# A two-layer graph network on one Trainium2 core: moving the low halves of two split operands ahead, and giving half of the last tile's evictions to ScalarE

## The chip, the cores and the metric

The kernel runs on one core of one Trainium2 chip. The engines that matter here are TensorE (PE in the profile, with its weight loads as PEld), VectorE (DVE), ScalarE (ACT) and GpSimd (POOL); SyncE (SP) issues most of the transfers. Each engine has its own queue of instructions, in the order in which the program emits them; an instruction may have to wait for the results of others, and those behind it on its engine wait with it. The metric is the time of one execution on the device in microseconds (us). The kernel before takes 777.34 us as the median of three runs.

## What is computed

Two graph layers over 2048 nodes, 8 batches and 64 channels, each followed by a residual and a layer norm. `A` is a sparse, row-normalised adjacency matrix.

```python
# layer 0: Chebyshev terms x, Ax, 2A(Ax) - x, mixed by weights that differ from node to node
w   = einsum('nd,dkio->nkio', embedding, weight)      # d = 16, k = 3
x_g = einsum('knm,bmc->bnkc', [I, A, 2AA - I], x)
x   = layernorm(x + einsum('bnki,nkio->bno', x_g, w) + embedding @ bias)
# layer 1: x, Ax, 2A(Ax) - x (twice, with the same A) through one shared weight
x   = layernorm(x + concat([x, Ax, 2AAx - x, Ax, 2AAx - x]) @ W + b)
```

The node-dependent weight is never formed. The kernel multiplies the three terms of a tile of 128 nodes by all 16 weight matrices at once, and then adds the 16 products, each scaled with the node's own embedding value.

## The kernel before

**The stages.** The two hops of layer 0 come first (226 us), then the mixing stage (316 us), which is what the change is about, and last the two hops of layer 1 (234 us). The first product of the first hop of layer 1 follows directly on the last tile of the mixing stage.

**The mixing stage** runs over 16 tiles of 128 nodes, `t` = 0 to 15 (the loop at line 819). A tile has two groups `g` of batches and four groups `dg` of weight matrices: eight pieces, called (0,0) to (1,3) here. For each piece `mix0` (line 393) emits 36 matmuls (line 415) into one buffer `pm` of the accumulator memory, and four scaled evictions that empty that buffer: pieces (0,0) and (1,0) by ScalarE into a buffer `aside` (line 425), whose four parts GpSimd then adds up (line 430), and the six other pieces by VectorE straight into the tile's sum `acc` (line 427). At (1,2) and at the end of the tile GpSimd adds the asides to `acc` (line 399). The tile's layer norm follows: VectorE takes the sum over channels (line 361), GpSimd subtracts the mean (364), ScalarE squares (352), VectorE sums the squares and refines a reciprocal root (369, 333 to 344), GpSimd multiplies (373).

**The accumulator memory** is four buffers (`bank`, line 84) that serve in turn for the eight pieces and for the transposes and projections between them. A piece can start only when the buffer it is given has been emptied. In the program as built, piece (0,0) of a tile gets the buffer of piece (1,2) of the tile before, and piece (0,1) that of (1,3); both are emptied by VectorE.

**The operands of a piece.** An fp32 factor is split into a high half (rounded by ScalarE, line 312), a low half (VectorE: source minus high half, line 314) and a mixed term (ScalarE scales, line 318, and GpSimd adds, line 319). `parts` (line 309) is a generator that does this in two steps: high half; then low half and mixed term. `operands(t)` (line 693) sets it up for the three factors of tile `t`: `of_x` from a transfer `xt` (line 696), `of_hop` from a transpose of `z[1][t]` on TensorE (line 710), `of_second` from `z[2][t]` (line 713), which `times_r` on GpSimd must have scaled before (line 683).

**The order around a tile** is written out by hand: the list `at[g, dg]` holds what is emitted just ahead of a piece's matmuls, and so ahead of its evictions. In tile `t` the factors of tile `t + 1` are prepared: hop at (0,2), x at (0,3) and (1,0), second at (1,1) and (1,2). The layer norm of tile `t - 1` is worked off at (0,2) and (0,3); its result is transposed at (1,3) and projected after the last piece (`project`, line 434: 16 matmuls at line 442, six copies by ScalarE at line 451). Only then does the next tile's first VectorE work come, the sum over channels.

**The last tile** (t = 15) has no next factors. In their place `early` (line 810) prepares steps 0 to 4 of the first product of the next stage: a high half (ScalarE, line 234), a low half (VectorE, line 238), a load of a matrix block (lines 607 to 613, by the helper at 123) and, for steps 0 and 1, its conversion by ScalarE (line 620). The projection of tile 14 comes between pieces (1,2) and (1,3).

**The pools.** The asides, the third factor's parts and the loaded blocks share five buffers ("raw"); the first two factors' parts share four ("s") with the converted blocks; the high halves have eight ("hl"), the transfers `xt` two.

## Time and profile before

| what | us |
|---|---|
| median of three runs (lowest, highest) | 777.34 (777.04, 777.93) |
| the profiled execution, its own time | 777.52 |
| its span, from the first to the last instruction | 775.6 |
| of it the stage 226.2 to 541.9 (mixing) | 315.7 |
| in that stage: PE / PEld / DVE / ACT / POOL busy | 309.8 / 305.3 / 271.2 / 153.1 / 218.3 |
| mean granted TensorE clock, share of full speed | 0.998 |

Spans and instruction times below are those of the profiled execution, which took 0.18 us more than the median. In a list of instructions the columns are start, duration, engine, line, operation, output and inputs, and, in brackets, the idle time of the engine ahead of it and who ended it. The ends of matmuls are modelled, so their starts say more than their durations.

### The profile page before, as it was taken

The page shows a single profiled execution, that of the slowest core. Times are in us where ns is not written, and L with a number is a line of the kernel's source. Part 1 is how long each engine was busy: PE and PEld are TensorE (multiplying, and loading weights), DVE is VectorE, ACT ScalarE, POOL GpSimd, SP SyncE. Part 2 cuts the span into 40 slices and gives each one's busy share as a digit, 9 for nine tenths or more (in the row PEclk, how much of TensorE's full clock was granted, in tenths as well). Part 3 has the DMA queues.
Part 4 walks back from the last instruction along what each step waited for, and adds up shares of the span by engine and source line. Part 5 has one row for each costly group of instructions (what it writes and reads, how often), then busy time and mean ns, then how long its engine had stood idle before and what let it go on. Part 6 is the DMA issues. An engine that isn't in the chain of part 4 may idle for free.

```text
span 775.6 us, 17992 instructions
## 1 busy us (share of the span) xinstructions
PE 761.5 (98%) x7246; PEld 675.2 (87%) x7246; DVE 590.7 (76%) x1230; ACT 386.5 (50%) x752; POOL 251.1 (32%) x245
## 2 busy tenths in 40 slices
PE   9999999999999999999999999999999999999996
PEld 6888888888889999999999999999888888888885
DVE  6778766677748888888888888888678747768663
ACT  4446443877753555544445444445787664112111
POOL 0000000000036777777777777763100000012341
PEclk9999999999999999999999999999999999999999
DMA  9998995655510000000000000011454444565731
GB/s 315 379 399 284 333 315 182 183 156 169 167 42 16 17 15 16 15 16 15 17 16 16 16 16 15 2 30 42 143 163 143 136 150 143 170 190 158 216 129 45
DMA packets 73546, 96.77 MB, mean 125 GB/s; under 512 B 4848, under 2 KB 48368, under 8 KB 73328
## 3 DMA queue, kind: packets, MB, share of 16 engines
q1 hardware_dynamic: 62048, 76.66, 31.5%
q10 hardware_dynamic: 11408, 18.89, 6.5%
q8 instruction: 59, 0.97, 0.5%
q14 instruction: 31, 0.25, 0.1%
HBM read 76.65 MB, written 18.87 MB: 123 GB/s over the span
## 4 chain that ended last, share of the span: by engine, by line
PE 69%; DVE 26%; issue 4%; POOL 0%; ACT 0%; DVEq 0%; POOLq 0%
PE accT L632 26%; DVE acc L427 18%; PE acc L254 15%; PE pm L415 10%; PE a L254 9%; PE accT L254 6%; DVE parts L314 3%; DVE ln_v L333 2%; DVE ss L369 1%; PE accT L782 1%; PE first L143 1%; DVE ln_q L341 0%; DVE ln_q L342 0%; DVE ln_r L344 0%; DVE ln_r L338 0%
## 5 line engine op out<-in xcount | busy, mean ns | idle before, releaser
L415 PE MATMUL pm<-wh,hl 64*128 64x256 f32 x1536 | 240.9, 286 | 5.9 <-DVE acc L427 5.9
L415 PE MATMUL pm<-wm,parts 64*128 64x256 f32 x1536 | 235.9, 280 | 0.0
L415 PE MATMUL pm<-wl,parts 64*128 64x256 f32 x1536 | 235.9, 280 | 0.0
L632 PE MATMUL accT<-s,hl 128*128 128x512 f32 x896 | 205.7, 390 | 0.0
L427 DVE SCALAR_TENSOR_TENSOR acc<-pm,pack_sb,acc 128x256 f32<-128x256 f32 x384 | 185.1, 482 | 26.3 <-PE pm L415 14.2
L632 PEld LDWEIGHTS accT<-s,hl 128*128 128x128 f32 x896 | 167.5, 188 | 35.4 <-issue 0.2
L415 PEld LDWEIGHTS pm<-wh,hl 64*128 64x128 f32 x1536 | 165.2, 188 | 10.6 <-DVE acc L427 8.8
L415 PEld LDWEIGHTS pm<-wl,parts 64*128 64x128 f32 x1536 | 165.2, 187 | 0.0
L415 PEld LDWEIGHTS pm<-wm,parts 64*128 64x128 f32 x1536 | 165.0, 187 | 0.0
L620 ACT CAST s<-raw 128x1024 fp32r<-128x1024 bf16 x104 | 109.7, 1055 | 38.2 <-ACT hl L234 23.5
L254 PE MATMUL acc<-hl,s 128*128 128x512 f32 x512 | 117.1, 390 | 0.0
L254 PEld LDWEIGHTS acc<-hl,s 128*128 128x128 f32 x512 | 95.7, 188 | 21.4 <-DVE hl L238 0.7
L683 POOL TENSOR_TENSOR z<-z,rrow 128x512 f32<-128x512 f32 x16 | 21.0, 1318 | 212.4 <-DVE z L656 212.4
L425 ACT ACTIVATE aside<-pm,pack_sb 128x256 f32<-128x256 f32 x128 | 50.3, 476 | 67.7 <-PE pm L415 67.7
L234 ACT CAST hl<-z 128x256 fp32r<-128x256 f32 (+1 forms) x96 | 47.5, 511 | 64.0 <-PE acc L254 23.4
L430 POOL TENSOR_TENSOR aside<-aside 128x512 f32<-128x512 f32 x64 | 69.8, 1090 | 16.2 <-ACT aside L425 13.7
L254 PE MATMUL a<-hl,s 128*128 128x512 f32 (+1 forms) x352 | 73.4, 370 | 0.0
L254 PEld LDWEIGHTS a<-hl,s 128*128 128x128 f32 x352 | 61.9, 188 | 11.3
L319 POOL TENSOR_TENSOR parts<-parts 128x512 fp32r<-128x512 f32 x45 | 58.0, 1289 | 16.6 <-DVE parts L314 16.0
L238 DVE TENSOR_TENSOR hl<-z,hl 128x512 fp32r<-128x512 f32 (+1 forms) x96 | 53.0, 559 | 10.6 <-ACT hl L234 8.0
L287 POOL TENSOR_TENSOR z<-z,got 128x512 f32<-128x512 f32 x3 | 4.8, 1622 | 143.8 <-ACT got L286 143.8
L254 PE MATMUL accT<-hl,s 128*128 128x512 f32 x192 | 44.3, 390 | 0.0
(129 smaller groups left out, 829.6 us busy)
## 6 DMA issues: line engine op xcount, KB each, us to landing
raw<-in_adj SPq DMA_DIRECT2D x59, 512.0 KB, 5.7
raw<-sums_of SPq DMA_DIRECT2D x64, 256.0 KB, 2.9
sums_of<-z ACTq DMA_DIRECT2D x16, 512.0 KB, 6.2
raw<-quarters SPq DMA_DIRECT2D x32, 256.0 KB, 2.8
raw<-in_adj SPq DMA_DIRECT2D x16, 384.0 KB, 3.4
quarters<-seen ACTq DMA_DIRECT2D x16, 256.0 KB, 5.6
xt<-in_xT SPq DMA_DIRECT2D x16, 256.0 KB, 2.8
z<-in_x SPq DMA_DIRECT2D x15, 256.0 KB, 6.9
```

The costliest lines, as they stand in the source:

```text
L234: ordered(nc.scalar.copy(to[0], src))
L238: ordered(nc.vector.tensor_tensor(to[1], src, to[0], ALU.subtract))
L254: nc.tensor.matmul(accs[i], lhsT=s[:, i * P : (i + 1) * P], rhs=hl[h], start=(first and h == 0), stop=(last and h == 1),)
L314: ordered(nc.vector.tensor_tensor(view(low), src, view(high), ALU.subtract))
L319: ordered(nc.gpsimd.tensor_tensor(mixed, mixed, low, ALU.add))
L415: nc.tensor.matmul(pm[:, j, i], lhsT=tt[k][n][q, 2 * g + i, :], rhs=w_parts[n][k][q, ds, :], start=(k == 0 and n == 0), stop=(k == 2 and n ...
L425: ordered(nc.scalar.activation(aside[g][:, d], got, AF.Copy, scale=e))
L427: ordered(nc.vector.scalar_tensor_tensor(part, got, e, part, ALU.mult, ALU.add))
L430: ordered(nc.gpsimd.tensor_tensor(aside[g][:, :n], aside[g][:, :n], aside[g][:, n : 2 * n], ALU.add))
L620: ordered(nc.scalar.copy(s, got["raw"]))
L632: nc.tensor.matmul(acc[i][:, c], lhsT=hl[h][:, i * P : (i + 1) * P], rhs=S[:, c * 512 : (c + 1) * 512], start=(kk == 0 and h == 0), stop=( ...
L683: ordered(nc.gpsimd.tensor_tensor(to, to, r, ALU.mult))
```

## The change

Three things are changed, all in the mixing stage.

1. `parts` yields once more, between the low half and the mixed term. The transfer `xt` of tile `t + 2` is issued at (1,0) of tile `t`; its high half (ScalarE) and low half (VectorE) are emitted after the projection at the end of tile `t`, ahead of that tile's sum over channels; its mixed term follows at (0,1) of tile `t + 1`. Tile 0 does all three steps for tile 1 at its piece (0,1).
2. The high half of the second factor is emitted at (0,3) instead of (1,1), its low half and mixed term at (1,0) instead of (1,2). The hop factor stays at (0,2).
3. In the last tile pieces (0,1) and (1,1) are evicted by ScalarE too (`on_act=2`): into a second aside, which GpSimd adds to the first. The first aside is added to `acc` ahead of (1,0). The second and third step of tile 14's norm come one piece later, the high and low halves of steps 0 to 4 are emitted at (0,1), (0,2), (0,3), (1,0) and (1,1), the loads of steps 2 to 4 are left to the next stage's own schedule, and the result of tile 14 is transposed at (1,2) instead of (1,3).

```diff
--- before.py
+++ after.py
@@ -312,6 +312,7 @@
         ordered(nc.scalar.copy(view(high), src))
         yield
         ordered(nc.vector.tensor_tensor(view(low), src, view(high), ALU.subtract))
+        yield
         if quick:
             ordered(nc.vector.scalar_tensor_tensor(mixed, high, 1.0 / SPLIT, low, ALU.mult, ALU.add))
         else:
@@ -390,7 +391,7 @@
             ))
         return acc
 
-    def mix0(t, tt, acc, at):
+    def mix0(t, tt, acc, at, on_act=1):
 
         aside = [None, None]
 
@@ -398,10 +399,13 @@
             part = acc[:, 4 * g : 4 * g + 4, :]
             ordered(nc.gpsimd.tensor_tensor(part, part, aside[g][:, 0], ALU.add))
 
+        def summed(one, other, n):
+            ordered(nc.gpsimd.tensor_tensor(one[:, :n], one[:, :n], other, ALU.add))
+
         for g in range(2):
             part = acc[:, 4 * g : 4 * g + 4, :]
             for dg in range(D // DG):
-                if (g, dg) == (1, 2):
+                if (g, dg) == (1, 2 if on_act == 1 else 0):
                     add_aside(0)
                 for work_here in at.get((g, dg), ()):
                     work_here()
@@ -416,18 +420,23 @@
                                     pm[:, j, i], lhsT=tt[k][n][q, 2 * g + i, :], rhs=w_parts[n][k][q, ds, :],
                                     start=(k == 0 and n == 0), stop=(k == 2 and n == 2),
                                 )
-                if dg == 0:
-                    aside[g] = rawp.tile([P, DG, B // 2, C], F32, tag="raw", name="aside")
+                if dg < on_act:
+                    to = rawp.tile([P, DG, B // 2, C], F32, tag="raw", name="aside")
                 for d in range(DG):
                     dd = dg * DG + d
                     got, e = pm[:, :, :, d, :].rearrange("p j i c -> p (j i) c"), emb_sb[:, t, dd : dd + 1]
-                    if dg == 0:
-                        ordered(nc.scalar.activation(aside[g][:, d], got, AF.Copy, scale=e))
+                    if dg < on_act:
+                        ordered(nc.scalar.activation(to[:, d], got, AF.Copy, scale=e))
                     else:
                         ordered(nc.vector.scalar_tensor_tensor(part, got, e, part, ALU.mult, ALU.add))
-                if dg == 0:
-                    for n in (2, 1):
-                        ordered(nc.gpsimd.tensor_tensor(aside[g][:, :n], aside[g][:, :n], aside[g][:, n : 2 * n], ALU.add))
+                if dg < on_act:
+                    if dg == 0:
+                        aside[g] = to
+                    else:
+                        summed(aside[g], to, DG)
+                    if dg == on_act - 1:
+                        for n in (2, 1):
+                            summed(aside[g], aside[g][:, n : 2 * n], n)
         add_aside(1)
         return layernorm(acc)
 
@@ -807,48 +816,56 @@
 
     third_got = {}
 
-    def early(i, least=0):
+    def early(i, *kinds):
 
         got = third_got.setdefault(i, {})
         for lead, part in sorted(third[i], key=lambda part: -part[0]):
-            if lead > least:
+            if part.__name__ in kinds:
                 part(got)
-        third[i] = [part for part in third[i] if part[0] <= least]
-
-    tt, acc, h, norm = first_tile[0], first_tile[5], None, None
+        third[i] = [part for part in third[i] if part[1].__name__ not in kinds]
+
+    def go(it):
+        return lambda: next(it)
+
+    y, s = ("y_high", "y_low"), ("load_sum", "operands")
+    acc, h, norm = first_tile[5], None, None
+    tt = first_tile[0]
+    coming = operands(1)
     for t in range(NT):
         got, last = {}, t == NT - 1
         at = {(g, dg): [] for g in range(2) for dg in range(D // DG)}
+        n1, n2, n3 = [lambda: next(norm)] * 3 if t else [nothing] * 3
 
         if not last:
-            got["tt"], of_x, of_hop, of_second = operands(t + 1)
+            following, of_x, of_hop, of_second = coming
             of_hop = of_hop()
-            at[0, 2] += [lambda it=of_hop: next(it), lambda: next(norm) if t else None, lambda it=of_hop: next(it)]
+            at[0, 1] += [go(of_x)] * (1 if t else 3)
+            at[0, 2] += [go(of_hop), n1, go(of_hop), go(of_hop), n2]
             if t + 2 < NT:
                 at[0, 2] += [lambda: times_r(t + 2)]
-            at[0, 3] += [lambda it=of_x: next(it), lambda: got.update(acc=begin_sum(t + 1))]
-            at[1, 0] += [lambda it=of_x: next(it)]
-            at[1, 1] += [lambda it=of_second: next(it)]
-            at[1, 2] += [lambda it=of_second: next(it)]
-        if t > 0:
-            if last:
-                at[0, 1] += [lambda: next(norm)]
-            at[0, 1 if last else 2] += [lambda: next(norm)]
-            at[0, 2 if last else 3].insert(0, lambda: next(norm))
-            at[1, 2 if last else 3] += [lambda: got.update(hT=transpose(h, "hT"))]
-        if last:
-            at[0, 1] += [lambda: early(0)]
-            at[0, 2] += [lambda: early(1)]
-            at[1, 0] += [lambda: early(2, 2)]
-            at[1, 1] += [lambda: early(3, 2)]
-            at[1, 2] += [lambda: early(4, 2)]
+                at[1, 0] += [lambda: got.update(coming=operands(t + 2))]
+            at[0, 3] += [n3, go(of_second), lambda: got.update(acc=begin_sum(t + 1))]
+            at[1, 0] += [go(of_second), go(of_second)]
+            at[1, 3] += [lambda: got.update(hT=transpose(h, "hT"))] if t else []
+        else:
+            at[0, 1] += [n1, lambda: early(0, *y, *s)]
+            at[0, 2] += [n2, lambda: early(1, *y, *s)]
+            at[0, 3] += [n3, lambda: early(2, *y)]
+            at[1, 0] += [lambda: early(3, *y)]
+            at[1, 1] += [lambda: early(4, *y)]
+            at[1, 2] += [lambda: got.update(hT=transpose(h, "hT"))]
             at[1, 3] += [lambda: project(t - 1, got["hT"])]
-        norm_now = mix0(t, tt, acc, at)
+        norm_now = mix0(t, tt, acc, at, 2 if last else 1)
         if 0 < t < NT - 1:
             project(t - 1, got["hT"])
+        if "coming" in got:
+            coming = got["coming"]
+            next(coming[1])
+            next(coming[1])
         norm = norm_now
         h = next(norm)
-        tt, acc = got.get("tt"), got.get("acc")
+        if not last:
+            tt, acc = following, got["acc"]
     todo.extend([nothing] * 4 + [lambda: next(norm)] * 3)
 
 
```

## The prediction

> **What bounds the kernel now.** I read the busy shares first, then who waits for whom, then one tile border and the last tile in order of time.
>
> ```profile
> PE 761.5 (98%) x7246; PEld 675.2 (87%) x7246; DVE 590.7 (76%) x1230; ACT 386.5 (50%) x752; POOL 251.1 (32%) x245
> ```
>
> TensorE is the bound over the whole span, so only gaps of TensorE can be won, and there are few. The waits say which, and for whom:
>
> ```profile
> DVE s L361 <- POOL acc L399: 14.9, 16, 1.2
> ...
> PEld pm L415 <- DVE acc L427: 8.8, 14, 0.7
> ...
> PE pm L415 <- DVE acc L427: 5.9, 15, 1.3
> ```
>
> (total us, times, longest.) Fourteen times, at 0.63 us each, TensorE waits for VectorE to empty a buffer. In order of time that is the border of two tiles, here the one at 402 us (TensorE alone):
>
> ```profile
> 400.42 0.31 PE L415 MATMUL pm<-wm,parts 64*128 64x256 f32 x2
> 400.55 1.49 PE L442 MATMUL pu<-v,hT 64*128 64x192 f32 x16
> 402.36 0.38 PE L415 MATMUL pm<-wh,hl 64*128 64x256 f32 x2 [0.33 <-DVE acc L427]
> 402.58 0.28 PE L415 MATMUL pm<-wl,parts 64*128 64x256 f32 x2
> 402.70 0.28 PE L415 MATMUL pm<-wm,parts 64*128 64x256 f32 x2
> ...
> 404.62 0.37 PE L415 MATMUL pm<-wh,hl 64*128 64x256 f32 x2
> 404.79 0.31 PE L415 MATMUL pm<-wl,parts 64*128 64x256 f32 x2
> ```
>
> A pair of matmuls starts every 0.12 us. The projection's 8 pairs take (1.49 - 0.32) / 7 = 0.17 us each, so the last starts at 401.72, and (0,0) could follow at about 401.87. It starts at 402.36, 0.49 late; the next pair comes after 0.22 instead of 0.12, and (0,1)'s second pair after 0.17. That makes 0.64, the 0.63 of the list. VectorE in the same tile:
>
> ```profile
> 393.93 2.03 DVE L427 SCALAR_TENSOR_TENSOR acc<-pm,pack_sb,acc 128x256 f32<-128x256 f32 x4
> 395.88 1.22 DVE L314 TENSOR_TENSOR parts<-xt,hl 128x512 fp32r<-128x512 f32 x1
> 397.02 2.03 DVE L427 SCALAR_TENSOR_TENSOR acc<-pm,pack_sb,acc 128x256 f32<-128x256 f32 x4
> 398.97 1.39 DVE L314 TENSOR_TENSOR parts<-z,hl 128x512 fp32r<-128x512 f32 x1
> 400.28 4.17 DVE L427 SCALAR_TENSOR_TENSOR acc<-pm,pack_sb,acc 128x256 f32<-128x256 f32 x8
> ```
>
> These are (0,3), low x, (1,1), low second, then (1,2) and (1,3) in one row. TensorE had finished (1,2) at about 398.1, before its transposes; VectorE empties it by 402.36, and at that moment (0,0) starts. VectorE is thus two microseconds late at a tile's end, but idle 0.9 us right after it (the mean's wait for GpSimd in the list above) and 0.8 us more ahead of (0,1). It isn't full; its work stands in the wrong place.
>
> The last tile has one longer gap:
>
> ```profile
> 534.40 0.46 PE L300 MATMUL pt<-ident,xc 64*128 64x64 f32 x8
> 536.11 0.39 PE L415 MATMUL pm<-wh,hl 64*128 64x256 f32 x2 [1.25 <-DVE acc L427]
> ```
>
> VectorE there empties (0,2), (0,3) and (1,1) with five low halves between them, and TensorE waits for (0,3).
>
> **What the Trainium skill says.** "Perfetto Trace Analysis", section Identifying the Most-Contended Engine, calls a busy share of matmuls a poor measure and takes that of weight loads. The trace agrees: PE is 98% busy at 0.31 us a pair that starts every 0.12, so I count starts. Its section Optimization Strategy says that the same gap repeated on the engine that should be saturated can mean too few buffers; here it repeats 14 times, and the buffers come free late because of VectorE's order. "GPSIMD Engine Reference", section 1, Specifications, says that GpSimd shares its SBUF interfaces with VectorE, with contention for VectorE instructions with two SBUF inputs. The trace agrees in size: the same 512-element subtraction takes 0.68 us from the transpose's buffer, but 1.15 for x and 1.34 for second, whose sources are both in SBUF and beside which GpSimd is at work.
>
> **Part 1, low x at the end of the tile.** Nothing is added: 16 instructions of line 314 in the stage before and after. Out of the middle of the tile go 1.14 us (395.88 to 397.02), so (1,1), (1,2) and (1,3) are emptied 1.14 us earlier as far as TensorE has filled them. The buffer of (0,0) then is free by 402.36 - 1.14 = 401.22, against 401.87 needed: slack 0.65. That of (0,1), now free at 404.45, is free at 403.3, against 401.87 + 2.16 = 404.03: slack 0.7.
>
> Low x now stands ahead of the mean and waits for its high half, which on ScalarE stands behind the projection's six copies. With T for the unstalled start of (0,0), 401.87, the copies (401.42, 1.75 long, and not sooner, since they follow the projection) end at T + 1.3, the high half (0.61) at T + 1.9. The last eviction ends at T + 1.4, so VectorE idles 0.5 there. Low x takes 0.68 to 1.39; I take 1.15, as GpSimd adds the aside beside it (0.74): to T + 3.1. The mean (0.69 + 0.17, and 0.1 of gaps) ends at T + 4.1. TensorE fills (0,1) by T + 4.4, so VectorE is still in time; at 1.39 just so. Then GpSimd subtracts to T + 5.2 and ScalarE squares to T + 6.3, behind the hop's high half as now; VectorE asks for the squares after the evictions of (0,1) and low hop, at T + 7.0. Behind the new waits stand the mean and (0,1) on VectorE, and aside (0,0) on ScalarE, ready only at T + 2.4: nothing late.
>
> On GpSimd the mixed x moves ahead of mixed hop. Its row from the norm's subtraction: 5.2, two sums 7.3, mixed x 8.6, mixed hop 9.9, times_r 11.2, the norm's product 12.3 (needed by the transpose at T + 15.6), the next sum's start 13.7. SP issues xt one tile sooner (2.8 us to land, over 7 there); nothing else stands in its queue in this stage, and the transfer's buffer was emptied a tile before. The pools don't bind: high halves need 7 of 8 buffers, and the parts' buffer was freed by the tile just evicted.
>
> **Part 2, second at (0,3) and (1,0).** On VectorE low second comes ahead of (1,1) instead of (1,2). It fills the place of low x and changes no sum; its partner on GpSimd is the next sum's start rather than the aside's sums. Duration 0.68 to 1.39; I keep 1.31 from start to start. The mixed term is on GpSimd by T + 16, where it stood as late as 1.3 us into the next tile before; ScalarE has been idle 2 us ahead of aside (1,0), so its 1.3 us cost nothing. Worth 0, or a few tenths of slack.
>
> VectorE's tile as placed: (0,1) at 4.5, low hop 6.5, squares 7.1, 7.8, (0,2) 8.5, root 10.5, (0,3) 11.2, low second 13.1, (1,1) 14.4, (1,2) 16.4, (1,3) 18.5 to 20.5, against a tile of 19.83 - 0.65 = 19.2. So (1,2) is empty at 18.4 of 19.2, and (1,3) at 20.5 of 21.4. Parts 1 and 2 take the whole gap: 14 x 0.63 = 8.8 us. Bounds: 0.5 a border if a change of operands still costs a refill (7.0), 0.69 at most, which is 19.83 less 144 pairs at 0.12, 8 at 0.17 and two transposes at 0.27 (9.6).
>
> **Part 3, the last tile.** Eight evictions (4 x 0.48 twice) go from VectorE to ScalarE at the same price (0.476 against 0.482). GpSimd gets two additions of 1024 elements, not in the trace: twice the 1.30 of 512 elements, 2.6 each; bounds 1.5 and 2.8. With T the tile's start: ScalarE evicts (0,0) to 3.9, squares to 5.0, high half and conversion to 6.2, evicts (0,1) to 7.8, high half 1 at 8.3. VectorE's low half 1 waits for that, (0,2) is emptied 8.7 to 10.7, root 11.4, low 2, (0,3) 11.8 to 13.7. TensorE has filled (1,1) at 13.3, then transposes: these wait for GpSimd, 7.9 + 2.6 + 1.3 + 0.85 + 1.05 = 13.7. The next piece needs (0,3) empty, 13.7. So the gap of 1.25 shrinks to some 0.4, and ScalarE, emptying (1,1) to 15.2, copies the transpose by 15.8, before (1,2) ends at 16.2. Worth 0.9; bounds 0 and 1.25. The loads of steps 3 and 4 now wait for GpSimd (about T + 15 and 18) and land 3 us later; their conversions are wanted 5 and 7 us into the next stage: covered. Were they not, each late conversion would cost TensorE its delay, 1 to 3 us in all.
>
> **Sum.** 777.52 - 8.8 - 0.9 = 767.8 in the profiled execution's own time; the median is 0.18 lower, so 767.6. The next stage is paced by TensorE too, so the shift lasts to the end.
>
> **The rivals.** *A, as worked out:* 767.6, own range 766.5 to 768.6. *B, the last tile stays as it was:* GpSimd's long additions and the ScalarE queue hold the transpose for 1.3 us more; for it speaks that the change fits with nothing to spare there, against it that 0.4 is already allowed. 777.34 - 8.8 = 768.5, up to 769.5 with a late load. *C, half the border gap comes back:* low x behind six copies and beside GpSimd ends later than T + 3.5, and (0,1) starts late; VectorE's slack of 0.65 absorbs the first part. At 0.3 a border: 777.34 - 4.2 - 0.9 = 772.2. *D, no change:* the buffer named in the list is not what holds TensorE, and another wait ends at the same instant; against it, (0,0) starts in the same hundredth in which (1,2) is empty, over and over. 777.3. *E, slower:* low x ahead of the mean. The mean, and with it (0,1) and all of VectorE's tile, waits for ScalarE's copies. Slack to T + 4.5 and then 0.65 are used up if low x ends 1.05 us later than placed, at T + 4.15; it equals today's gap at T + 4.8, and from there every microsecond is lost at 14 borders. At T + 5.2 that is 14 x 0.4 = 5.6, less 0.9: 782.0. It would need 3.3 us for an operation that the trace shows at 1.39 at most.
>
> **How the numbers follow.** A 0.70, B 0.12, C 0.11, D 0.03, E 0.04. This measurement can tell about 0.2% (1.6 us) from no change. Faster 0.93, same 0.03, slower 0.04. The range leaves out D, E and most of C; its lower end is the larger bounds of parts 1 to 3 (9.6 + 1.25 below 777.34 gives 766.5, with 0.2 for repetition), its upper end B and the smaller bound of the borders: 766.3 to 770.0.
>
> **What would show it.** Right: in the list of waits TensorE's loads no longer wait for line 427's successor at tile borders, tiles start every 19.2 us, the mean no longer waits 0.9 for GpSimd, and VectorE waits for TensorE ahead of (0,1). Wrong: a wait of VectorE for ScalarE's high half of x of over 1 us; pairs of TensorE that wait for GpSimd or ScalarE; a first conversion after the stage that comes late.

## The result, and the profile after

The changed kernel takes 769.22 us (median of five runs, 768.66 to 770.68), the kernel before, beside it on the same chip, 777.34 (777.04 to 777.93). The ratio is 0.9897, with a 95% interval of 0.9883 to 0.9912: 8.1 us, or 1.0%, faster. The profiled execution of the changed kernel took 768.76 us, with a span of 767.0; the one before took 777.52, so the pair that the traces compare differ by 8.76. The first line of the page, engines by busy time:

```profile
PE 757.0 (99%) x7246; PEld 674.8 (88%) x7246; DVE 582.8 (76%) x1222; ACT 387.7 (51%) x760; POOL 252.5 (33%) x247
```

Eight instructions have gone from VectorE to ScalarE (1230 to 1222, 752 to 760), and GpSimd has two more; that is part 3. The list of waits (total us, times, longest) shows what happened to the gap:

```profile
DVE s L362 <- POOL acc L400: 3.7, 5, 0.9
...
PE pt L300 <- POOL xc L374: 0.9, 1, 0.9
...
PE pm L419 <- DVE acc L431: 0.7, 1, 0.7
```

The row of 14 waits of TensorE's loads for VectorE is gone (line 427 of before is line 431 here), and the 15 waits of its matmuls are now one, in the last tile. There is a new one beside it, of the transposes for GpSimd. The mean's wait for GpSimd, 14.9 us in 16 times before, is 3.7 in 5. A tile border in order of time (TensorE alone, the border at 397 us):

```profile
396.31 0.30 PE L419 MATMUL pm<-wm,parts 64*128 64x256 f32 x2
396.44 1.49 PE L451 MATMUL pu<-v,hT 64*128 64x192 f32 x16
397.63 0.41 PE L419 MATMUL pm<-wh,hl 64*128 64x256 f32 x2
397.86 0.30 PE L419 MATMUL pm<-wl,parts 64*128 64x256 f32 x2
```

Piece (0,0) follows the projection after 1.19 us and without an idle time in brackets; before it was 1.81 and stood in brackets with 0.33.

Where the 8.76 us come from, with a tile counted from the first matmul of its (0,0):

| stretch | before | after | difference |
|---|---|---|---|
| start of the mixing stage | 226.24 | 226.81 | +0.57 |
| tiles 0 and 1 | 37.31 | 36.74 | -0.57 |
| tiles 2 to 14, 13 of them | 257.76 (19.83 each) | 248.98 (19.15 each) | -8.78 |
| last tile, to the next stage's first product | 20.60 | 21.11 | +0.51 |
| from there to the end of the execution's own time | 235.61 | 235.12 | -0.49 |

The borders gave 9.35 us (the second and third rows), a little more than was forecast. The last tile became longer where it was to become shorter. The first and the last row are not put down to the change: in the thirteen kernels profiled here, whose first stage is the same, the start of the mixing stage moved between 226.01 and 226.84, and the stretch of the last row between 235.09 and 236.16.

Now the last tile. TensorE waits twice in it (TensorE alone):

```profile
526.71 0.46 PE L300 MATMUL pt<-ident,xc 64*128 64x64 f32 x8 [0.91 <-POOL xc L374]
527.85 0.39 PE L419 MATMUL pm<-wh,hl 64*128 64x256 f32 x2 [0.69 <-DVE acc L431]
```

VectorE in the same stretch:

```profile
520.50 2.25 DVE L238 TENSOR_TENSOR hl<-z,hl 128x256 fp32r<-128x256 f32 x1 [1.67 <-ACT hl L234]
522.67 2.03 DVE L431 SCALAR_TENSOR_TENSOR acc<-pm,pack_sb,acc 128x256 f32<-128x256 f32 x4
...
525.25 0.17 DVE L345 SCALAR_TENSOR_TENSOR ln_r<-ln_q,ln_r 128x8 f32<-128x8 f32 x1
525.34 0.42 DVE L238 TENSOR_TENSOR hl<-z,hl 128x256 fp32r<-128x256 f32 x1
525.67 2.04 DVE L431 SCALAR_TENSOR_TENSOR acc<-pm,pack_sb,acc 128x256 f32<-128x256 f32 x4
```

And GpSimd, whose first instruction here is the new addition, of 1024 elements, in one row with the two sums behind it:

```profile
520.06 4.66 POOL L403 TENSOR_TENSOR aside<-aside 128x1024 f32<-128x1024 f32 x3 [3.45 <-ACT aside L429]
525.50 1.16 POOL L374 TENSOR_TENSOR xc<-xc,ln_r 128x512 f32<-128x512 f32 x1 [0.78 <-DVE ln_r L345]
```

One line stands out: low half 1 of the next stage took 2.25 us at 520.50, and the same operation took 0.42 at 525.34. It lies in GpSimd's addition. All that is queued behind it on VectorE is late with it: (0,2) is emptied from 522.67, the root ends at 525.4, GpSimd's product of the norm can start only at 525.50, the transposes get it at 526.7, and (0,3), emptied last, holds the next piece to 527.85.

### The profile page after: what moved, and what is told of

It reads as the page before. It is cut to its first block, busy times and chain, and to the rows that moved or that the text cites. A ratio compares the mean times of both kernels' runs of the same rounds, so it can differ in the third digit from the quotient of the medians.

```text
span 767.0 us, 18011 instructions
## 1 busy us (share of the span) xinstructions
PE 757.0 (99%) x7246; PEld 674.8 (88%) x7246; DVE 582.8 (76%) x1222; ACT 387.7 (51%) x760; POOL 252.5 (33%) x247
## 4 chain that ended last, share of the span: by engine, by line
PE 96%; DVE 2%; DMA 1%; ACT 1%; POOL 0%; issue 0%; SPq 0%; POOLq 0%; DVEq 0%
PE pm L419 35%; PE accT L641 27%; PE acc L254 15%; PE a L254 10%; PE accT L254 6%; PE pu L451 2%; DMA raw<-in_adj 1%; PE pt L300 1%; DVE acc L431 1%; PE accT L791 1%; DVE hl L238 0%; PE accT L451 0%; ACT aside L429 0%; SPq L123 0%; POOL xc L365 0%
## 5 line engine op out<-in xcount | busy, mean ns | idle before, releaser
L419 PE MATMUL pm<-wh,hl 64*128 64x256 f32 x1536 | 235.4, 286 | 0.7 <-DVE acc L431 0.7
L419 PE MATMUL pm<-wm,parts 64*128 64x256 f32 x1536 | 230.9, 280 | 0.0
L419 PE MATMUL pm<-wl,parts 64*128 64x256 f32 x1536 | 230.8, 280 | 0.0
L431 DVE SCALAR_TENSOR_TENSOR acc<-pm,pack_sb,acc 128x256 f32<-128x256 f32 x376 | 181.5, 483 | 27.5 <-PE pm L419 14.1
L419 PEld LDWEIGHTS pm<-wh,hl 64*128 64x128 f32 x1536 | 160.3, 188 | 1.2 <-PE pt L300 0.8
L419 PEld LDWEIGHTS pm<-wl,parts 64*128 64x128 f32 x1536 | 160.2, 188 | 0.0
L419 PEld LDWEIGHTS pm<-wm,parts 64*128 64x128 f32 x1536 | 160.0, 187 | 0.0
L429 ACT ACTIVATE aside<-pm,pack_sb 128x256 f32<-128x256 f32 x136 | 53.3, 475 | 54.0 <-PE pm L419 54.0
L403 POOL TENSOR_TENSOR aside<-aside 128x512 f32<-128x512 f32 (+2 forms) x66 | 70.5, 1068 | 18.4 <-ACT aside L429 15.7
L238 DVE TENSOR_TENSOR hl<-z,hl 128x512 fp32r<-128x512 f32 (+1 forms) x96 | 54.6, 576 | 14.0 <-ACT hl L234 11.4
```

Source lines behind the costliest of these rows:

```text
L238: ordered(nc.vector.tensor_tensor(to[1], src, to[0], ALU.subtract))
L403: ordered(nc.gpsimd.tensor_tensor(one[:, :n], one[:, :n], other, ALU.add))
L419: nc.tensor.matmul(pm[:, j, i], lhsT=tt[k][n][q, 2 * g + i, :], rhs=w_parts[n][k][q, ds, :], start=(k == 0 and n == 0), stop=(k == 2 and n ...
L429: ordered(nc.scalar.activation(to[:, d], got, AF.Copy, scale=e))
L431: ordered(nc.vector.scalar_tensor_tensor(part, got, e, part, ALU.mult, ALU.add))
```

## The experiments

Each kernel was timed beside the kernel before, on three later occasions (its median there 777.2 to 777.5). Edits are shown against the changed kernel. The lengths of tiles are from the one profiled execution of each, so a last tile is a single reading.

| kernel | median (lowest, highest) | ratio, 95% interval | a tile | last tile |
|---|---|---|---|---|
| before | 777.34 (777.04, 777.93) | | 19.83 | 20.60 |
| the change | 769.22 (768.66, 770.68) | 0.9897 (0.9883, 0.9912) | 19.15 | 21.11 |
| parts 1 and 2 | 767.50 (766.62, 767.80) | 0.9872 (0.9856, 0.9889) | 19.15 | 19.69 |
| part 1 alone | 767.75 (767.38, 768.18) | 0.9872 (0.9856, 0.9889) | 19.15 | 20.09 |
| part 2 alone | 770.29 (770.09, 771.29) | 0.9908 (0.9892, 0.9925) | 19.30 | 20.60 |
| part 3 alone | 779.49 (778.84, 780.65) | 1.0031 (1.0018, 1.0044) | 19.82 | 22.12 |
| 1, 2 and part 3's order | 767.81 (767.51, 768.08) | 0.9874 (0.9858, 0.9891) | 19.15 | 20.26 |
| 1, 2 and part 3's evictions | 770.51 (770.40, 770.75) | 0.9908 (0.9892, 0.9925) | 19.15 | 22.86 |
| low halves 1 and 2 later | 767.31 (766.66, 767.57) | 0.9870 (0.9854, 0.9887) | 19.15 | 19.97 |
| addition in two halves | 767.68 (767.21, 768.04) | 0.9878 (0.9861, 0.9894) | 19.15 | 20.01 |
| 1, 2, low half 1 later | 768.19 (768.04, 768.33) | 0.9878 (0.9862, 0.9895) | 19.15 | 20.57 |
| low x three times | 780.85 (779.72, 781.48) | 1.0041 (1.0027, 1.0055) | 19.86 | 23.27 |
| low x five times | 799.63 (798.53, 800.91) | 1.0286 (1.0269, 1.0304) | 21.30 | 22.11 |

### The parts, one at a time

**Parts 1 and 2 without part 3.** The last tile has its list and its evictions of before.

```diff
-            at[0, 1] += [n1, lambda: early(0, *y, *s)]
-            at[0, 2] += [n2, lambda: early(1, *y, *s)]
-            at[0, 3] += [n3, lambda: early(2, *y)]
-            at[1, 0] += [lambda: early(3, *y)]
-            at[1, 1] += [lambda: early(4, *y)]
-            at[1, 2] += [lambda: got.update(hT=transpose(h, "hT"))]
+            at[0, 1] += [n1, n2, lambda: early(0, *y, *s)]
+            at[0, 2] += [n3, lambda: early(1, *y, *s)]
+            at[1, 0] += [lambda: early(2, *y, "load_sum")]
+            at[1, 1] += [lambda: early(3, *y, "load_sum")]
+            at[1, 2] += [lambda: got.update(hT=transpose(h, "hT")), lambda: early(4, *y, "load_sum")]
...
-        norm_now = mix0(t, tt, acc, at, 2 if last else 1)
+        norm_now = mix0(t, tt, acc, at)
```

> Parts 1 and 2 kept, part 3 undone (the last tile's list and evictions as before). My theory, that part 3 costs 0.5 us and parts 1 and 2 bring all the gain: tiles every 19.15 us, the last tile (from its first matmul to the first one of the next stage) 20.4 to 20.6 us instead of 21.11, median about 768.7. Rival, that part 3 is neutral and the 0.5 us is a knock-on of parts 1 and 2 in that tile: the last tile stays near 21.1 and the median at 769.2.

Measured: 767.50, and the last tile 19.69, shorter than either theory had it. This kernel is faster than the changed one: its slowest run (767.80) is below the changed kernel's fastest (768.66), although the two were timed on different occasions and the intervals of their ratios still overlap a little (0.9889 and 0.9883). So part 3 costs 1.42 us in the last tile, 1.7 by the medians, and parts 1 and 2 alone shorten that tile by 0.91. (Tile 14's result is transposed at (1,2) here; in the kernel before it stood there too, so the move from (1,3) that the list of the change names is none.) The trace says how the tile got shorter. VectorE's mean in the last tile, before and here:

```profile
524.32 0.69 DVE L361 TENSOR_REDUCE s<-acc 128x8 f32<-128x512 f32 x1 [0.92 <-POOL acc L399]
```

```profile
514.24 0.69 DVE L362 TENSOR_REDUCE s<-acc 128x8 f32<-128x512 f32 x1 [0.92 <-POOL acc L400]
```

The tile starts at 521.31 before and at 512.22 here, so the mean comes 3.01 us after (0,0) before and 2.02 after it here, because VectorE is no longer late when the tile begins. The wait of 1.25 for (0,3) is down to 0.3 (waits of TensorE for VectorE):

```profile
PE pm L419 <- DVE acc L431: 0.3, 1, 0.3
```

The gap that part 3 was to close came for the most part from the same lateness of VectorE as the 14 borders, and went with it; part 2 alone, below, tells the two apart.

**Part 3 alone.** The loop over the tiles has its order of before, and the last tile is the changed one.

```diff
...
-            at[0, 1] += [go(of_x)] * (1 if t else 3)
...
-            at[0, 3] += [n3, go(of_second), lambda: got.update(acc=begin_sum(t + 1))]
-            at[1, 0] += [go(of_second), go(of_second)]
+            at[0, 3] += [n3, go(of_x), lambda: got.update(acc=begin_sum(t + 1))]
+            at[1, 0] += [go(of_x), go(of_x)]
+            at[1, 1] += [go(of_second)]
+            at[1, 2] += [go(of_second), go(of_second)]
...
-        if "coming" in got:
-            coming = got["coming"]
-            next(coming[1])
-            next(coming[1])
```

> Part 3 alone on the kernel before. My theory: tile borders keep their 0.63 us gap (tiles every 19.83 us), the last tile takes about 0.5 us longer than the 20.60 of before, median about 777.8. Rival, that part 3 is a gain by itself (0.9 us as predicted) and only clashes with part 1: last tile 19.7, median 776.4.

Measured: 779.49, slower than before in the whole interval of its ratio, and by more than my theory had. The tiles are those of before, and the last tile is 1.52 longer. Part 3 is a loss of the same size with and without parts 1 and 2.

**Part 3 divided.** First only its order (the call of `mix0` without the 2, so that VectorE keeps all evictions), then only its evictions (the last tile's list of before, `mix0` with the 2).

```diff
-        norm_now = mix0(t, tt, acc, at, 2 if last else 1)
+        norm_now = mix0(t, tt, acc, at)
```

> Parts 1 and 2 as in the changed kernel, and of part 3 only the order of the last tile (norm one piece later, low halves one piece sooner, loads left to the next stage, transpose at (1,2)); VectorE keeps (0,1) and (1,1), so GpSimd has no addition of 1024 elements. My theory (of the 1.4 us that part 3 costs, nearly all is the long GpSimd addition beside low half 1): last tile 19.6 to 20.1 us, median 767.4 to 768.0, low half 1 within 0.1 of 0.43. The rival (the order costs it: the norm's second and third step one piece later make the transposes wait): last tile 20.7 or more, median 768.6 or more.

> Parts 1 and 2 as in the changed kernel, and of part 3 only the evictions: (0,1) and (1,1) on ScalarE with GpSimd's additions of 1024 elements, the rest of the last tile in the order of before. My theory: low half 1 still falls beside GpSimd's long addition and lasts 1.5 to 2.3 us, last tile 20.7 to 21.3, median 768.7 to 769.4. The rival (the order costs it): last tile 19.5 to 20.0, median 767.4 to 767.9.

Measured: the order alone makes the last tile 20.26, 0.57 over the 19.69 of parts 1 and 2, a little outside what either theory had, and low half 1 takes its free 0.42. The evictions alone make the tile 22.86, beyond both theories, and low half 1 took 2.44 us, in the same place as in the changed kernel. So the evictions cost more than the order. Some of the 22.86 is the clock: in that execution TensorE was granted less right after its two gaps (columns: stretch; PE, PEld, DVE, ACT and POOL busy with counts; clock; share and rate of the transfers):

```profile
526.00:529.00 3.00, 1.37 (x22) 1.27 (x24) 2.89 (x6) 0.10 (x1) 1.60 (x2) 0.96 0.00 0
529.00:533.00 4.00, 4.00 (x41) 4.00 (x41) 1.86 (x2) 2.54 (x8) 2.37 (x2) 0.60 0.02 4
```

At 0.60 for four microseconds 1.6 us are lost; without them the tile would be about 21.2, 1.5 over the 19.69. Two of this kernel's four runs have a mean clock of 0.998, with little room for such a dip, and are as long (770.41 and 770.75). What made those long isn't in a trace. So it stays open whether the new order softens what the evictions cost: the medians say so (769.22 for both together, 770.51 for the evictions alone), the traces without the dip don't (21.11 and 21.2).

**Part 1 alone.** Second keeps its old places.

```diff
-            at[0, 3] += [n3, go(of_second), lambda: got.update(acc=begin_sum(t + 1))]
-            at[1, 0] += [go(of_second), go(of_second)]
+            at[0, 3] += [n3, lambda: got.update(acc=begin_sum(t + 1))]
+            at[1, 1] += [go(of_second)]
+            at[1, 2] += [go(of_second), go(of_second)]
```

The last tile is also that of before, as in the first experiment.

> Part 1 alone (low x at the end of the tile; second where it was, last tile as before). My step: taking 1.14 us out of the middle of VectorE's tile is what frees (1,2) in time, and part 2 changes no sum: tiles every 19.15 to 19.25 us, median about 767.5 to 769. Rival, part 2 is needed (low second at (1,2) still stands ahead of (1,2)'s evictions, 1.34 us long beside GpSimd): a gap of 0.2 to 0.6 us stays at each border, median 770 to 775.

Measured: 767.75 and tiles of 19.15. Part 1 alone closes every border. Its last tile, 20.09, is 0.40 longer than that of parts 1 and 2; by the medians the two can't be told apart.

**Part 2 alone.** x keeps its old places at (0,3) and (1,0), the transfer is not issued earlier, and second follows x directly.

```diff
...
-            at[0, 3] += [n3, go(of_second), lambda: got.update(acc=begin_sum(t + 1))]
-            at[1, 0] += [go(of_second), go(of_second)]
+            at[0, 3] += [n3, go(of_x), go(of_second), lambda: got.update(acc=begin_sum(t + 1))]
+            at[1, 0] += [go(of_x), go(of_x), go(of_second), go(of_second)]
...
```

The last tile is again that of before.

> Part 2 alone (second at (0,3) and (1,0), x where it was). My step: the same instructions stand ahead of (1,2)'s evictions in another order, so the border gap stays: tiles every 19.7 to 19.85 us, median 775.5 to 777.5. Rival, low second beside GpSimd's later sums was the costly part: tiles near 19.2, median under 770.

Measured: 770.29, and tiles of 19.30: four fifths of the border gap are gone, where I had expected it to stay. VectorE's order around (1,1) shows why:

```profile
411.69 1.21 DVE L314 TENSOR_TENSOR parts<-xt,hl 128x512 fp32r<-128x512 f32 x1
412.82 0.68 DVE L314 TENSOR_TENSOR parts<-z,hl 128x512 fp32r<-128x512 f32 x1
413.42 6.32 DVE L431 SCALAR_TENSOR_TENSOR acc<-pm,pack_sb,acc 128x256 f32<-128x256 f32 x12
```

Low second takes 0.68 instead of 1.39. It reads the same operands; only its place is another. When it starts there, no GpSimd instruction is at work: one ended at 412.35, the next starts at 413.06. GpSimd's row:

```profile
410.89 1.46 POOL L387 TENSOR_TENSOR acc<-z,ebias 128x256 f32<-128x256 f32 x2
```

The 0.71 saved a tile is about the size of the gap, 0.68. What is left is 0.15 a tile: (1,2) is emptied at 417.59, and (0,0), which needs its buffer, starts at 417.65.

The last tile stayed at 20.60, though most of the gap at its border is gone. VectorE's mean starts in it 3.01 us after (0,0), as before; with part 1 alone it is 2.50 (last tile 20.09), with both parts 2.02 (19.69). So the last tile is shorter by about as much as VectorE begins it sooner, and what it inherits is VectorE's lateness, not TensorE's gap.

### What a low half waits for

The lengths of the two-input operations of VectorE look arbitrary in the list of groups. They are not, once GpSimd is laid beside them. The two rows of GpSimd that lie beside low x and low second in the prediction's view of before:

```profile
395.09 1.46 POOL L386 TENSOR_TENSOR acc<-z,ebias 128x256 f32<-128x256 f32 x2
...
398.52 2.44 POOL L430 TENSOR_TENSOR aside<-aside 128x512 f32<-128x512 f32 x2
```

The second instruction of the first row ends at 396.55, low x at 397.10: 0.55 later. The first instruction of the second row ends at 399.81, low second at 400.36: 0.55 later. In the changed kernel's last tile the addition of 1024 elements ends at 522.47, low half 1, of 256 elements, at 522.75: 0.28 later. So the VectorE instruction waits until the GpSimd instruction at work ends, and then takes its own time (0.68 and 0.42 alone), less some 0.13 to 0.15. Three experiments put this to the test.

**The low halves of steps 1 and 2 behind the evictions of (0,3).**

```diff
-            at[0, 2] += [n2, lambda: early(1, *y, *s)]
-            at[0, 3] += [n3, lambda: early(2, *y)]
-            at[1, 0] += [lambda: early(3, *y)]
+            at[0, 2] += [n2, lambda: early(1, "y_high", *s)]
+            at[0, 3] += [n3, lambda: early(2, "y_high")]
+            at[1, 0] += [lambda: early(1, "y_low"), lambda: early(2, "y_low"), lambda: early(3, *y)]
```

> The changed kernel, with the low halves of steps 1 and 2 in the last tile behind VectorE's evictions of (0,3) instead of ahead of (0,2) and (0,3). Theory of the lock: a VectorE instruction with two SBUF inputs waits until the GpSimd instruction at work has ended, so low half 1, beside the addition of 1024 elements, held the evictions of (0,2) for 2 us; moved, (0,2) is emptied about 1.5 us sooner, (0,3) by 12 us into the tile, one of the two gaps of the last tile (0.7 us) goes and the other (1.1 us, the transpose's wait for GpSimd) stays or shrinks to some tenths: last tile 19.3 to 20.2 us, median 767.4 to 768.3. Rival, ScalarE's or GpSimd's queue as the bound (high half 1 behind the evictions of (0,1); the three additions ahead of the norm's product): the transpose still waits 1.1 us and the last tile stays within 0.5 us of 21.1.

Measured: 767.31, the lowest median of all, though not to be told from the 767.50 of parts 1 and 2, and a last tile of 19.97, 1.14 shorter than in the changed kernel. (0,2) is now emptied from 518.99, ahead of the long addition. But VectorE's root, behind it, falls into that addition:

```profile
518.99 2.04 DVE L431 SCALAR_TENSOR_TENSOR acc<-pm,pack_sb,acc 128x256 f32<-128x256 f32 x4
520.95 0.19 DVE L339 RECIPROCAL ln_r<-ln_sd 128x8 f32<-128x8 f32 x1
521.18 1.43 DVE L342 SCALAR_TENSOR_TENSOR ln_q<-ln_r 128x8 f32<-128x8 f32 x1
522.64 0.17 DVE L343 TENSOR_TENSOR ln_q<-ln_q,ln_v 128x8 f32<-128x8 f32 x1
522.85 1.15 DVE L345 SCALAR_TENSOR_TENSOR ln_r<-ln_q,ln_r 128x8 f32<-128x8 f32 x1
```

Operations on eight elements, 0.17 us elsewhere, take 1.43 and 1.15. GpSimd's instructions end at 522.58 and 523.97, these at 522.61 and 523.99. The reciprocal, with one input, and the evictions, with one of theirs in the accumulator memory, run beside the same addition at their usual lengths. It is not the amount of data that waits, but the instruction.

**The addition of 1024 elements as two of 512.** Nothing is moved.

```diff
-                        summed(aside[g], to, DG)
+                        for c in (slice(0, DG // 2), slice(DG // 2, DG)):
+                            ordered(nc.gpsimd.tensor_tensor(aside[g][:, c], aside[g][:, c], to[:, c], ALU.add))
```

> The changed kernel, with each of GpSimd's two additions of 1024 elements cut into two of 512. Theory of the lock: low half 1 of the last tile waits for 1.3 us at most in place of 2.5, so it takes about 1.3 instead of 2.25 us, (0,2) is emptied some 0.9 us sooner, and the last tile takes about 20.4 us; the GpSimd sums themselves end 0.2 to 0.5 us later. Rival, a slower VectorE instruction for a reason of its own (both engines slowed in proportion to the overlap): the low half keeps about 2 us, last tile 21.1 or more.

Measured: 767.68, last tile 20.01, and low half 1, in the same place on VectorE:

```profile
519.86 0.43 DVE L238 TENSOR_TENSOR hl<-z,hl 128x256 fp32r<-128x256 f32 x1 [1.67 <-ACT hl L234]
520.20 2.04 DVE L431 SCALAR_TENSOR_TENSOR acc<-pm,pack_sb,acc 128x256 f32<-128x256 f32 x4
```

GpSimd's row, the two halves of the addition:

```profile
518.69 2.74 POOL L437 TENSOR_TENSOR aside<-aside 128x512 f32<-128x512 f32 x2 [2.72 <-ACT aside L429]
```

The first half ends at 519.99, the low half at 520.28, 0.29 later: 0.43 us instead of 2.25, although the two halves take longer than the whole did. It was less than the 1.3 us expected, since the first half needs only two of ScalarE's four evictions and so starts 0.7 us sooner in the tile; the low half met its last 0.13 us. That the sums also ended sooner isn't what moved the tile: in both kernels GpSimd's product of the norm starts right behind VectorE's root (525.50 and 523.74). So the run changes both the length and the start of what the low half meets, and nothing on VectorE. It is the closest test of the cause, and it brings 1.10 of the 1.42 us.

**Low half 1 behind (0,3), without part 3.** An attempt at a still better kernel, from the first experiment's.

```diff
-            at[0, 2] += [n3, lambda: early(1, *y, *s)]
-            at[1, 0] += [lambda: early(2, *y, "load_sum")]
+            at[0, 2] += [n3, lambda: early(1, "y_high", *s)]
+            at[1, 0] += [lambda: early(1, "y_low"), lambda: early(2, *y, "load_sum")]
```

> Parts 1 and 2 without part 3, and low half 1 of the last tile emitted behind (0,3)'s evictions. If the 0.3 us for which (1,0) or its successor still waits for VectorE there is VectorE's order, the last tile goes from 19.7 to 19.4 and the median to 767.0 to 767.4; if the low half only takes its place in a later stretch beside GpSimd, it stays at 19.6 to 19.8 and 767.4 to 767.8.

Measured: worse than either expectation, 768.19 and a last tile of 20.57. The three low halves now stand together, beside GpSimd's sums, and TensorE's wait went from piece (1,2) to (1,3), and grew (VectorE, then TensorE):

```profile
525.44 2.92 DVE L238 TENSOR_TENSOR hl<-z,hl 128x256 fp32r<-128x256 f32 x3
```

```profile
530.38 0.39 PE L419 MATMUL pm<-wh,hl 64*128 64x256 f32 x2 [0.99 <-DVE acc L431]
```

Of the 2.92, 1.16 are the first of the three, which ends 0.28 after GpSimd's sum does (526.60 and 526.32). In its old place it took 0.42. A move that frees one stretch of VectorE can cost more where it lands.

### How much room VectorE has left

Low x is computed three times over, and then five times, with the same result each time: one and two pairs of further subtractions a tile, in the new place.

```diff
-        ordered(nc.vector.tensor_tensor(view(low), src, view(high), ALU.subtract))
+        for _ in range(1 + again):
+            ordered(nc.vector.tensor_tensor(view(low), src, view(high), ALU.subtract))
...
-            yield from begin(0, xt)
+            yield from begin(0, xt, 2 if t > 1 else 0)
```

(4 in place of 2 in the second kernel.)

> The changed kernel with low x computed three times over for tiles 2 to 15 (two more VectorE subtractions of about 0.6 us ahead of the mean, the result the same). By the trace of the changed kernel VectorE idles 0.64 + 0.47 us around the mean and has some 0.45 us more until (0,0) needs its buffer: 1.2 us more fit, if GpSimd's addition gets in between: tiles every 19.15 to 19.4 us, median 769 to 773. Rival, the slower case of the prediction (the mean behind low x decides at once): each added microsecond is lost at once, tiles every 20.3 us, median about 785.

> As before it, with low x five times over (four more, 2.4 us). About 1.55 us are free, so 0.9 us a tile are lost, and up to 0.7 more if GpSimd's addition waits for the whole row: tiles every 20.0 to 20.8 us, median 781 to 792. Rival, VectorE has far more room than placed: tiles under 19.5.

Measured: tiles of 19.86 and 21.30, medians 780.85 and 799.63; both are slower than my theory had them, and slower than the kernel before. The second pair costs 1.44 a tile, all the time of two more subtractions there (three take 2.56 us, five 4.01). The first pair costs 0.71, but by way of GpSimd, as these rows of VectorE with three times low x show:

```profile
413.51 0.37 DVE L343 SCALAR_TENSOR_TENSOR ln_q<-ln_r 128x8 f32<-128x8 f32 x1
413.91 1.22 DVE L344 TENSOR_TENSOR ln_q<-ln_q,ln_v 128x8 f32<-128x8 f32 x1
```

The root has slid beside the scaling of second (line 693 of that kernel, 413.80 to 415.10), and an operation on eight elements ends at 415.13. Tile 14 is the check on this. It has the same three low x, and its (0,1) is emptied from the same 5.28 us after its start, but no scaling on GpSimd, which prepares the second factor two tiles ahead and has no tile 16 to prepare:

```profile
512.83 0.34 DVE L343 SCALAR_TENSOR_TENSOR ln_q<-ln_r 128x8 f32<-128x8 f32 x1
513.21 0.17 DVE L344 TENSOR_TENSOR ln_q<-ln_q,ln_v 128x8 f32<-128x8 f32 x1
```

That tile takes 19.17, 0.69 less than the others; with five low x it takes 20.26, 1.04 less than the others. So without that one hold the first pair fits into the tile, with 0.44 us to spare; with it, the room is used up.

The trace of the changed kernel has the room, too: in the tile at 397 us (1,2) is emptied at 416.49, and the (0,0) that takes its buffer starts at 416.80, a slack of 0.3 us. It differs from tile to tile with the holds that VectorE meets: 0.05 to 1.18 in tiles 1 to 14, 0.6 in the median. The last tile of 23.27 with three times low x is no measure of room: TensorE waits in it for 1.54 and 0.68 us, and its clock was 0.61 in the four microseconds behind.

## Why the prediction came out as it did

**The median, 767.6 forecast and 769.2 measured, lies in the range, in part by luck.** The prediction's likeliest case, A, did not happen as worked out (its own range ended at 768.6); the time is near that of B, which names GpSimd's long additions, but has them hold the transpose, and not VectorE.

**Borders: right in mechanism and nearly in size.** Forecast 14 x 0.63 = 8.8, measured 9.35, or 0.67 each, within the bounds of 7.0 to 9.6 as they were stated. (The upper one doesn't follow from its own sum: 19.83 less 144 x 0.12, 8 x 0.17 and 2 x 0.27 is 0.65 a border and not 0.69; the measured 0.67 lies above it by no more than the rounding of these figures. And the range's upper end, B with the smaller bound of the borders, is 770.3 and not 770.0.) The tile was forecast at 19.2 and is 19.15. Low x as placed behind the six copies did no harm: in the fourteen tiles that have it there, its wait for ScalarE's high half is at most 0.79. VectorE waits for TensorE ahead of (0,1) as forecast, 0.47 in the tile at 397 us.

**The slack: a single figure for what differs from tile to tile.** The forecast had (1,2) empty 0.8 us ahead of its next use; it was 0.05 to 1.18, 0.6 in the median. In the tile at 397 us it was 0.3: against the forecast's list of VectorE's tile, (0,1) started at 4.68 instead of 4.5, the root took 0.97 instead of 0.7, since one of its operations on eight elements took 0.42 beside GpSimd, and (1,2) was empty at 18.86 instead of 18.4. It cost next to nothing in this change, but what else would fit into the tile could not be judged without the holds.

**"It fills the place of low x and changes no sum" (part 2): wrong.** Alone it saves 0.53 us a tile, since in its new place, behind low x, low second no longer meets GpSimd. Beside part 1 it has nothing left to close in the steady tiles (19.15 with and without it), and in the changed kernel low second meets the next sum's start and takes 1.21 again. So the value that I took, 0 or a few tenths, was right only because part 1 came with it; there the last tile is 0.40 shorter with part 2 than without (19.69 and 20.09, one reading each).

**Part 3, "Worth 0.9; bounds 0 and 1.25": wrong in sign.** It costs 1.42 (last tile 21.11 against 19.69) and 1.52 alone. Two steps failed.

- "VectorE's low half 1 waits for that, (0,2) is emptied 8.7 to 10.7": I gave the low half its free length, 0.42, beside an addition that I had myself placed at 7.9 to 10.5. It waited for the addition to end, and (0,2) was emptied from 10.1 to 12.2. From there all followed in the step's own order: the root was 1.5 us late and (0,3) empty at 15.2 instead of 13.7; the transposes started at 14.2 instead of 13.7, so (0,3) held the next piece last. The addition itself was well estimated: 2.6 forecast, 2.48 measured as the mean of two. The prediction had named contention, but as a surcharge, taken from the mean rows of operations of another length. The Trainium skill has the rule, in "SBUF — State Buffer", section Summary: rules for kernel authors, which I had not used: where a VectorE instruction has two SBUF inputs while GpSimd's reads SBUF, "the second one to issue **fully blocks** until the first finishes". This trace agrees: the low half ended 0.28 us after the addition, which is its own 0.42 but for some 0.14 that lie ahead of the wait. With it the step gives 7.9 + 2.6 + 0.3 = 10.8 for the end of the low half, two microseconds after the 8.7 that I wrote, and the 0.9 is gone before any run. Of the 1.42 the hold is 1.10, by the run with the addition cut in two. The new order alone costs 0.57 (20.26), so once the hold is gone the evictions bring 0.25 back (20.01); what in the order costs was not divided further.
- "So the gap of 1.25 shrinks to some 0.4": the gap was taken as the last tile's own. It came in large part from VectorE's lateness at the last border, and parts 1 and 2 took 0.91 by themselves. A wait of 0.3 was left for part 3.

In the sum the errors went against each other: borders 0.55 better than forecast, part 3 and the last tile together 1.4 worse (+0.51 in place of -0.9), the rest near zero. That is 0.9 in the profiled execution; the other 0.6 is that it ran 0.46 faster than the median, where 0.18 slower was forecast. In the last tile parts 1 and 2 saved the 0.9 that part 3 was to save, and part 3 then lost 1.42; that the first covered most of the second is luck. The rivals C, D and E are ruled out by the tiles of 19.15.

**The loads** of steps 3 and 4, left to the next stage, cost nothing that can be seen: the stretch after the mixing stage is 0.5 shorter than before, not longer, and no longer than in the kernels that keep these loads early (235.12, against 235.34 with parts 1 and 2).

## What to carry to other kernels

Don't price a VectorE operation with two SBUF inputs by its mean; lay GpSimd's queue beside it, and give it the end of the instruction that it meets plus its own length, less some 0.14 us. Long GpSimd instructions are then the dear ones: moving evictions from VectorE to another engine buys nothing if the sum that they need makes GpSimd hold VectorE for two microseconds, and cutting that sum in two gave most of it back. And before a second gap is attacked, ask whether it is the first one's shadow: here parts 1 and 2, which end VectorE's lateness at the borders, also took most of the last tile's gap, and part 2 alone, which closed most of the borders but left VectorE as late, took nothing of it.

## What the runs showed of the hardware

- The hold has a fixed end, and of the sizes only VectorE's own matters. In the thirteen traces, from 200 to 545 us, 639 VectorE instructions with two inputs in SBUF started with at least 0.14 us of a GpSimd instruction still to come, and without an exception they ended 0.55 us after it with 512 elements in each partition, 0.28 to 0.29 with 256, and 0.02 to 0.03 with 8, whether GpSimd's instruction took 0.7 or 2.6 us. Alone they take 0.68 to 0.69, 0.42 and 0.17, so some 0.14 us of each lies ahead of the wait. The longest single cost was 2.2 us (2.60 for a subtraction of 0.42, at 527.43 with the low halves 1 and 2 later).
- It goes both ways, with the order of starting: low x started 0.23 us ahead of GpSimd's addition at 399.87 in the changed kernel and took 0.68, and the addition took 1.06 in place of 0.73. It too was held for what was left of the other, 0.45, less 0.13. In the next tile the addition started 0.01 ahead, and low x took 1.28.
- Operations with one input, those with an input in the accumulator memory, and those that started just ahead of a GpSimd instruction kept their lengths (0.19, 0.48 and 0.68 us, and 0.17).
- In two of the thirteen profiled executions two TensorE gaps in the last tile were followed by about 4 us of a granted clock of 0.60 and 0.61: gaps of 1.05 and 0.76 us with the evictions alone, of 1.54 and 0.68 with three times low x. In the changed kernel (0.91 and 0.69) and with part 3 alone (1.91 and 0.68) they were followed by none. What decides it stays open. With part 3 alone three runs at a mean clock of 0.999 took 778.84 to 778.89 and three at 0.996 to 0.997 took 780.09 to 780.65; such a dip may be what divides them, but only one of the six has a trace.
